# Causal attention on Trainium2: transfers as jobs of their own, in a four-stage transformer block

## The chip, the cores and the metric

The kernel runs on one core of one Trainium2 chip. The metric is device time in microseconds of one execution; the median of the runs is compared. The core's engines are called PE (TensorE, matmuls), DVE (VectorE), ACT (ScalarE), POOL (GpSimd) and SP (SyncE, which here only issues DMAs). Each works through its own instructions in the order in which the program gives them, and waits at an instruction until what it needs is done.

## The reference

The block is a chain of residual stages on x of shape (2, 2048, 256), 4096 tokens of 256 features in float32. Cut to what matters:

```
x = x + 0.5 * moe(layernorm(x))            # mixture of 6 experts, top 2, and a shared expert
x = x + attention0(layernorm(x))           # 16 heads of 16, dense, 2048 x 2048 per head
x = x + 0.5 * moe(layernorm(x))            # the same weights again
x = x + 0.5 * rnn(layernorm(x))            # gated recurrence, then an output projection
x = x + attention1(layernorm(x))           # 16 heads of 16, causal, rotary, relative positions
x = x + 0.5 * rnn(layernorm(x))

def attention1(x):
    q, k = rotary(x @ w_q.T), rotary(x @ w_k.T);  q = q / 4;  v = x @ w_v.T
    rel  = rel_emb[clip(k_pos - q_pos, -32, 32) + 32]          # (L, L, 16)
    s    = q . k  +  q . rel                                   # per head
    a    = softmax(where(k_pos <= q_pos, s, -1e18))
    return (a @ v + sum_k a * rel) @ w_o.T
```

The relative part differs from a constant only in the last 32 keys in front of each query, so the kernel treats a band of 160 columns per 128 queries by itself.

## The kernel before

The token axis is cut into blocks of 512 (TB), of which each batch row has four (SB, named qc for queries), each of four pieces of 128 (CPB, named qb). Heads are taken four at a time (J = 4; G = 4 groups), each in its own 32 rows of PE. One unit of attention work, a group, is (b, qc, g): 32 groups in all. PE writes its products into eight PSUM banks that are handed out in turn by `bank()`, so an engine that is late with emptying a bank stops PE.

*Mixture stages* (`run_moe`). A list written out by hand gives the order of the jobs: `stats(n)` (layer norm statistics on DVE, their reciprocal root on POOL, L96 to L98), `norm(n)` (normalising on DVE, L109, and transposing on PE, L119), `scatter(n)` (eight indirect DMAs issued by POOL, L311, that carry tokens to the places of their experts), `up`, `mul` and `down` for the shared expert. POOL's order is kept as written (`tc.manual_schedule`).

*Attention 0.* A table of jobs by step. Step −1 holds the key products of the first batch row (`keys`: two matmuls on PE, a copy on ACT at L691, eight spread DMAs and eight padding DMAs on SP), then follow, two units per step, `largest` (products of L716 and a row maximum on DVE, L720), and nine steps later `exponential` (L728 on PE, L733 on ACT) and `weighted` (L740 on PE, `gather` at L606 to L611). `vals` computes the values (eight matmuls at L578 for each of eight tiles of a batch row, copied by ACT at L584). For the first row they are jobs of steps 6 to 9.

*`gather`* copies a partial product out of PSUM on ACT (`part`) and adds it to the accumulator `o` on POOL (L611). The first part of a group goes straight into `o`.

*Recurrence* (`recurrence`): the jobs of the layer norm that follows run among its steps.

*Attention 1.* A planner writes lists of steps: `Ms` to `Me` for `largest` of a group (L1055, L1063, L1079), `Es` to `Ee` for its exponentials, `Rs` for its positional product, `By` for the earliest step of its band. Jobs are placed by these. The pieces:

- `rotate` (L960 to L976): a projection on PE, a copy to an `s2` buffer on ACT (L968), a partner swap on DVE (`stream_shuffle`, L970), and multiplications by cos and sin on POOL (L972 to L976). There are four `s2` buffers, shared with other tiles of that size.
- `spread` (L134): eight or four small DMAs on SP that put packed heads into their 32-row groups. `queries` rotates and spreads in one job; `keys` rotates and `keys_out` spreads, both at the same step. `pad_keys` (L141) fills the rest of the rows. The 48 padding DMAs of the later chunks stand before the first step.
- `by_position`: query times relative embedding (L1018), copied by ACT (L1023), stored to DRAM by SP (`skew`, L1025) and loaded back shifted by one column per row (`band`, L1032) in the same job.
- `largest` works on the band (POOL memset L1076 for the first chunk, DVE L1079), takes the maxima off it on POOL (L1093), and with the last of its pieces stores the band to DRAM (`pd`, L1101).
- `positions_load` (L1178) loads the band back unshifted, `positions_exp` (L1186) is its exponential on ACT, `positions_T` and `positions` (L1191, L1197) multiply it by the relative embedding.

All DMAs named here are issued by SP, in the order in which the jobs stand:

```
at(max(By[n], early[n - n % 2] + 2), by_position, n)
at(Rs[n] - 3, positions_load, n)
at(Rs[n] - 2, positions_exp, n)
```

Within a step, half of its jobs run behind the first unit of work and half behind the second.

Of the kernel before, what the change touches and what calls it, by code (L numbers as in the profile page):

```python
# [10 lines left out]
F32 = mybir.dt.float32  # L11
# [6 lines left out]
P = 128  # L18
# [7 lines left out]
TB = 512  # L26
NTB = NT // TB
CPB = TB // P
# [14 lines left out]
def macaron_kernel(ctx: ExitStack, tc: tile.TileContext, t: dict, out: bass.AP):  # L43
    nc = tc.nc
# [121 lines left out]
    def moe(w, ws, gate_w, gate_b, rev, tri, iota, z, behind, last, gathered):  # L166
# [3 lines left out]
        with ExitStack() as s:  # L170
# [14 lines left out]
            def stats(b):  # L185
                if b not in xn and b not in z.mv:
                    z.stats(b)
# [252 lines left out]
            with tc.manual_schedule(engines={mybir.EngineType.Pool}):  # L440
                stats(0)
                stats(1)
                norm(0)
                stats(2)
                norm(1)
                shared_part(0, 0)
                shared_part(0, 1)
                stats(3)
                norm(2)
                shared_part(0, 2)  # L450
                norm(3)
                shared_part(0, 3)
                mul(0)
                stats(4)
                route(0)
                up(1)
                e0 = sort(0)
                stats(5)
                down(0)
                scatter(0)  # L460
                mul(1)
                up(2)
                stats(6)
                up(3)
                scatter(1)
                mul(2)
                norm(4)
                norm(5)
                stats(7)
                scatter(2)  # L470
                scatter(3)
                down(1)
                mul(3)
                down(2)
                norm(6)
                norm(7)
                down(3)
                route(1)
                up(4)
                mul(4)  # L480
                e1 = sort(1)
                down(4)
                up(5)
                mul(5)
                for b in range(HB, NTB):
                    scatter(b)
                down(5)
# [12 lines left out]

                rest(2)
                up(7)
                mul(7)
                rest(1)
                down(6)
                rest(1)
                down(7)
                rest(4)
                if gathered is None:
                    rest(HC)  # L510
# [13 lines left out]
    class Pieces:  # L524
# [76 lines left out]

        def gather(self, t, pv, parts, q0=0):

            if t not in self.o:
                self.o[t] = self.wk.tile([P, TB], F32, name="o")
                nc.scalar.copy(self.o[t], pv)  # L606
                return
            part = self.wk.tile([P, TB], F32, name="part", bufs=parts)
            nc.scalar.copy(part[:, q0:], pv[:, q0:])  # L609
            o = self.o[t][:, q0:]  # L610
            nc.gpsimd.tensor_tensor(o, o, part[:, q0:], ALU.add)  # L611

# [47 lines left out]
    def attention0(norm, tail, wq, wk_, wv, wo, bff):  # L660
# [7 lines left out]
        with ExitStack() as s:  # L668
# [82 lines left out]
            for b in range(B):  # L751
                first = b * SB * G * PER

                for qc in range(SB) if b else ():
                    for c in range(CPB):
                        at(first - 43 + 4 * qc + c, z.ln_stats, b, qc, c)
                    at(first - 37 + 4 * qc, z.ln_transpose, b, qc)
                for qc in range(0 if b else SB):
                    norm.xn.pop(qc)
                    at(-1, z.add_bias, qc)  # L760
                for g in range(0, G, 2):
                    for qc in range(SB):
                        at(first - 7 + PER * g + qc if b else -1, keys, b, g, qc)
                for half in range(2):
                    for qc in range(SB):
                        due = first + 1 + 16 * half + qc
                        at(due if b else 6 + half * 2 + qc // 2, vals, b, half, qc)
            for t, (b, qc, g) in enumerate(groups):
                if t % 2 == 0:
                    at(PER * t - 2, queries, t)  # L770
# [161 lines left out]
    def attention1(norm, tail, w, relk, relv, kbias, dramp, skew):  # L932
# [4 lines left out]
        with ExitStack() as s:  # L937
# [43 lines left out]
            for qc in range(1, SB):  # L981
                for g in range(G):
                    keep_k[qc, g] = z.keep.tile([P, TB], F32, name=f"kT{qc}{g}")
                    pad_keys(keep_k[qc, g])

            def keys(b, qc, g):
                if qc == 0:
                    pair = features_slot()
                for i in range(2):
                    k = kT[b, qc, g + i] = keep_k[qc, g + i] if qc else pair[:, i, :]  # L990
                    if qc == 0:
                        pad_keys(k)
                packed[b, qc, g] = rotate(w["k"], b, qc, g, kbias)

# [7 lines left out]
            def queries(t):  # L1002
                b, qc, g = groups[t]
                z.clear_queries(t)
                xa = rotate(w["q"], b, qc, g, None)
                for i in range(2):
                    spread(q[t + i], xa, i)
                    mx[t + i] = wk.tile([P, CPB, J, MX], F32, name="mx", bufs=2)

            def by_position(t):  # L1010

# [5 lines left out]
                for qb in range(CPB):  # L1017
# [4 lines left out]
                u = wk.tile([P, CPB * J, BAND], F32, name="s2", bufs=4)  # L1022
                nc.scalar.copy(u.rearrange("p a d -> p (a d)"), pr)  # L1023
                flat = skew[t % len(skew)]
                nc.sync.dma_start(  # L1025
                    out=flat.rearrange("s (r w) -> r s w", w=UW)[:, :, P : P + BAND], in_=u
                )
                lead[t] = leads[t % NBAND]
                c = band[t] = lead[t][:, P - BAND :].rearrange(
                    "p (a j k) -> p a j k", a=CPB, j=J  # L1030
# [16 lines left out]
            def largest(t, qb, c, j):  # L1047
# [46 lines left out]
                    band[t][:, qb], band[t][:, qb],  # L1094
                    mneg[:, :, DH : DH + 1].to_broadcast([P, J, BW]), ALU.add,
                )
                if qb < CPB - 1:
                    return

                pd[t] = dramp.tile([CPB * J, P * (BW + 1) + 1], F32, name="pd")  # L1100
                nc.sync.dma_start(  # L1101
# [100 lines left out]
            for n, (b, qc, g) in enumerate(groups):  # L1202
                size = 2 * (qc + 1)
                start = Me[-1] + 1 if n else 0
                free = Es[n - NBAND] + (4 if groups[n - NBAND][1] else 2) if n >= NBAND else -9
                start = max(start, free + 4 - size)
                if n > 5 and n % 2 == 0:
                    start = max(start, Ee[n - 5] + 4)
                Ms.append(start)
                Me.append(start + size - 1)  # L1210
                By.append(max(free, start - 3))
                start = Me[-1] + 2
                if n:
                    start = max(start, Ee[-1] + 1)
                Es.append(start)
                Ee.append(start + size - 1)
                Rs.append(start + (3 if size == 2 else 4))
            largest_at, exp_at = Jobs(), Jobs()
            for n, (b, qc, g) in enumerate(groups):
                for i, piece in enumerate(pieces(qc)):  # L1220
                    largest_at.at(Ms[n] + i // 2, None, n, *piece)
# [3 lines left out]
            at = jobs.at  # L1225
            index = {x_: n for n, x_ in enumerate(groups)}
            early = {
                n: max(Ms[n] - 6, Ee[n - 5] + 1) if n > 5 else Ms[n] - 6 for n in range(0, NG, 2)
            }
            for n in range(NG):  # L1230
                at(Me[n] + 1, z.subtract, n)
            for n in early:
                at(early[n], queries, n)
            for b in range(B):
                for qc in range(SB):
                    f = Ms[index[b, max(qc, 1), 0]]
# [3 lines left out]
                    at(max(f - 12, free), tables, b, qc)  # L1240
                    if b or qc > 1:
                        for c in range(CPB):
                            at(f - 14 + c, z.ln_stats, b, qc, c)
                        at(f - 8, z.ln_transpose, b, qc)
                    for g in range(0, G, 2):
                        f = Ms[index[b, max(qc, 1), g]]
                        at(f - 6 + (qc == 0), keys, b, qc, g)
                        for i in range(2):
                            last_ = Ee[index[b - 1, SB - 1, g + i]] if b and qc else -99
                            at(max(f - 6 + (qc == 0), last_ + 1), keys_out, b, qc, g, i)  # L1250
                    for half in range(2):
                        due = Es[index[b, max(qc, 1), 2 * half]] - 1 + (qc == 0)
                        at(due if b or qc > 1 or half else -2, vals, b, qc, half)
            for n, (b, qc, g) in enumerate(groups):
                at(max(By[n], early[n - n % 2] + 2), by_position, n)
                at(Rs[n] - 3, positions_load, n)
                at(Rs[n] - 2, positions_exp, n)
                at(Rs[n] - 1, positions_T, n)
                at(Rs[n], positions, n)
                end = max(Rs[n], Ee[n] + 1)  # L1260
# [9 lines left out]
            for step in range(min(jobs), max(jobs) + 1):  # L1270
                exps = [a for _, a in exp_at.get(step, ())]
                maxs = [a for _, a in largest_at.get(step, ())]
                todo = jobs.get(step, [])
                for n in range(2):
                    e = exps[n] if n < len(exps) else None
                    m = maxs[n] if n < len(maxs) else None
                    qb = e[1] - groups[e[0]][1] * CPB if e is not None else -2
# [82 lines left out]
    with tc.manual_schedule(engines=ENGINES):  # L1360
# [21 lines left out]
        with ExitStack() as s:  # L1382
# [35 lines left out]
                    n4.turn(cb - 2)  # L1418
                    n4.xn.pop(cb - 2)

            recurrence(rec, n3, False, rest, normals, turns)
        tail = []
        for i, b in enumerate((0, SB)):
            tail += [(3 + 2 * i, n5.stats, b), (4 + 2 * i, n5.normal, b, nc.vector),
# [84 lines left out]
```

## Time and profile before

| | |
|---|---|
| time, median of 3 runs (lowest to highest) | 4228.29 us (4227.61 to 4237.52) |
| profiled execution: its own time, its span | 4239.39 us, 4237.5 us |
| granted PE clock, mean of the span | 0.974 |
| PE busy | 4045.4 us (95%) |
| DVE, ACT, POOL busy | 2696.1, 2499.4, 1696.8 us |

The stages lie one behind the other in the trace: the first mixture at 0 to 420 us, attention 0 at 420 to 2060, the second mixture to 2435, the first recurrence to 2623, attention 1 at 2623 to 4046, and the second recurrence to the end. Times in the trace count from the start of the span. A bracket behind an instruction, such as `[6.42 <-DVE xn L109]`, gives the idle time of its engine before it and the instruction whose end released it. SPq stands for SP's sequencer, which issues DMAs. An instruction has the line of the kernel as printed above; the changed kernel's lines shift by up to 14.

### The profile page before, as it was taken

The numbers are of one execution on the slowest core, as the hardware profiler recorded it, in microseconds if no ns is written. First come the engines' busy times: TensorE is split into PE (matmuls) and PEld (weight loads), VectorE is DVE, ScalarE is ACT, GpSimd is POOL, SyncE is SP. The second block draws the span as 40 slices with busy tenths as digits, with TensorE's granted clock in tenths as the row PEclk, the third lists the DMA queues.
The fourth block names the chain that finished last, engine by engine and source line by source line (L and its number), as shares of the span: only waits on it lengthen the run. The fifth ranks groups of instructions, "written<-read, shape, count | busy, mean of one in ns | idle before, by whom it ended". The sixth has DMA issues, their size and how long they took to land. (4 is left out here: it accounts for less than half of the span.)

```text
span 4237.5 us, 78186 instructions
## 1 busy us (share of the span) xinstructions
PE 4045.4 (95%) x28256; PEld 1952.4 (46%) x28256; DVE 2696.1 (64%) x6122; ACT 2499.4 (59%) x5091; POOL 1696.8 (40%) x1606
## 2 busy tenths in 40 slices
PE   7998999999999999999999988898899999999999
PEld 4664433333344333333356645454454455554445
DVE  6245788888776888888543344665566665666633
ACT  2331788888877888888723231355556665656832
POOL 4244243446333433343362210535535655543510
PEclk9998999999999999999999999899999999999999
DMA  7343000000000000000334201535523444442201
GB/s 245 120 125 86 15 4 4 4 4 4 6 11 14 4 4 4 4 4 12 111 125 126 88 19 36 116 74 100 113 58 65 93 84 100 85 101 41 46 22 40
DMA packets 376881, 245.36 MB, mean 58 GB/s; under 512 B 157232, under 2 KB 349104, under 8 KB 376496
## 3 DMA queue, kind: packets, MB, share of 16 engines
q1 hardware_dynamic: 364208, 206.78, 20.1%
q0 software_dynamic: 12288, 33.57, 2.5%
q8 instruction: 226, 3.70, 0.4%
q14 instruction: 159, 1.30, 0.1%
HBM read 118.36 MB, written 105.12 MB: 53 GB/s over the span
## 5 line engine op out<-in xcount | busy, mean ns | idle before, releaser
L611 POOL TENSOR_TENSOR o<-o,part 128x512 f32<-128x512 f32 (+3 forms) x800 | 964.2, 1206 | 1447.3 <-ACT part L609 1439.4
L720 DVE TENSOR_REDUCE mx<-s 128x1 f32<-128x512 f32 x2048 | 1270.5, 683 | 306.9 <-PE s L716 306.8
L733 ACT ACTIVATE pT<-s 128x512 f32<-128x512 f32 x2048 | 1063.5, 617 | 196.3 <-PE s L716 195.6
L716 PE MATMUL s<-kT,q 32*128 32x512 f32 x4096 | 1030.3, 623 | 11.2 <-DVE mx L720 10.4
L728 PE MATMUL s<-q,kT 32*128 32x512 f32 x4096 | 1011.4, 614 | 0.0
L1161 ACT ACTIVATE pT<-s 128x512 f32<-128x512 f32 (+3 forms) x1280 | 589.8, 541 | 246.3 <-PE s L1140 124.6
L728 PEld LDWEIGHTS s<-q,kT 32*128 32x128 f32 x4096 | 417.3, 183 | 464.4 <-DVE mx L720 325.3
L609 ACT COPY part<-s 128x512 f32<-128x512 f32 (+3 forms) x800 | 467.3, 585 | 277.4 <-PE s L1169 160.4
L1063 DVE TENSOR_REDUCE mx<-s 128x1 f32<-128x512 f32 (+1 forms) x768 | 473.2, 678 | 211.6 <-PE s L1055 190.8
L740 PE MATMUL s<-pT,v 128*32 128x512 f32 x4096 | 549.9, 605 | 0.4
L716 PEld LDWEIGHTS s<-kT,q 32*128 32x128 f32 x4096 | 415.5, 185 | 146.3 <-ACT pT L733 78.3
L1055 PE MATMUL s<-kT,q 32*128 32x160 f32 (+7 forms) x2240 | 339.9, 441 | 22.9 <-ACT part L609 21.5
L1169 PE MATMUL s<-pT,v 128*32 128x512 f32 (+3 forms) x2560 | 313.6, 558 | 22.8 <-DVE mx L1079 13.2
L376 PE MATMUL s<-we,xT 128*128 x592 | 278.9, 593 | 1.1 <-ACT xT L371 1.1
L1079 DVE CUSTOM_DVE_ANT_0 band<-s,band 128x160 f32<-128x160 f32 (+1 forms) x512 | 155.4, 315 | 178.3 <-PE s L1055 76.7
L383 DVE TENSOR_TENSOR h<-sg,s 128x256 f32<-128x256 f32 x148 | 62.3, 421 | 294.8 <-ACT sg L381 294.8
L1055 PE MATMUL s<-b,q 32*128 32x512 f32 (+7 forms) x1280 | 244.3, 520 | 3.5 <-ACT part L609 2.0
L1140 PE MATMUL s<-q,kT 32*128 32x512 f32 (+3 forms) x1152 | 238.9, 512 | 0.0
L740 PEld LDWEIGHTS s<-pT,v 128*32 128x32 f32 x4096 | 82.1, 108 | 335.3 <-ACT pT L733 297.6
L1093 POOL TENSOR_TENSOR band<-band,mneg 128x640 f32<-128x640 f32 x128 | 161.4, 1262 | 174.8 <-DVE mneg L1089 172.4
L423 POOL DMA_INDIRECT yg<-results,at x128 | 125.1, 977 | 239.0 <-DMA results<-y 110.1
L1140 PE MATMUL s<-q,b 32*128 32x512 f32 (+3 forms) x896 | 219.0, 583 | 0.2 <-DVE mx L1079 0.2
(208 smaller groups left out, 5201.1 us busy)
## 6 DMA issues: line engine op xcount, KB each, us to landing
band<-skew SPq DMA_DIRECT2D x32, 1280.0 KB
pd<-band SPq DMA_DIRECT2D x32, 1280.0 KB
xs<-places SPq DMA_DIRECT2D x148, 128.0 KB
results<-y SPq DMA_DIRECT2D x148, 128.0 KB
places<-zero SPq DMA_DIRECT2D x2, 4736.0 KB
we<-in_we SPq DMA_DIRECT2D x12, 768.0 KB
skew<-s SPq DMA_DIRECT2D x32, 256.0 KB
s<-pd SPq DMA_DIRECT2D x32, 256.0 KB
```

The costliest lines, as they stand in the source:

```text
L609: nc.scalar.copy(part[:, q0:], pv[:, q0:])
L611: nc.gpsimd.tensor_tensor(o, o, part[:, q0:], ALU.add)
L716: nc.tensor.matmul(ps, lhsT=q[t][rows(j), ts(qb, P)], rhs=kT[b, g][rows(j), ts(kc, TB)], start=True, stop=True,)
L720: nc.vector.tensor_reduce(mx[t][:, qb * J + j, kc : kc + 1], ps, AX.X, ALU.max)
L728: nc.tensor.matmul(st, lhsT=kT[b, g][rows(j), ts(kb, P)], rhs=q[t][rows(j), :], start=True, stop=True,)
L733: nc.scalar.activation(z.pTs[t, kb, j], st, AF.Exp)
L740: nc.tensor.matmul(pv[rows(j), :], lhsT=v[b, g // 2][:, kb, ds(h * VW, 32)], rhs=z.pTs.pop((t, kb, j)), start=True, stop=True,)
L1055: nc.tensor.matmul(ps[:, ds(cols, n)], lhsT=lhsT, rhs=kT[b, c, g][rows(j), ds(k0, n)], start=True, stop=True,)
L1063: nc.vector.tensor_reduce(m[:, c : c + 1], ps[:, 0:n], AX.X, ALU.max)
L1140: nc.tensor.matmul(ps[:, q0:], lhsT=k, rhs=q[t][rows(j), q0:], start=True, stop=True, skip_group_check=True,)
L1161: nc.scalar.activation(z.pTs[t, kb, j][:, q0:], st.pop((t, kb, j))[:, q0:], AF.Exp)
L1169: nc.tensor.matmul(pv[rows(j), q0:], lhsT=v[b, kb // CPB, g // 2][:, kb % CPB, ds(h * VW, 32)], rhs=z.pTs.pop((t, kb, j))[:, q0:], start=T ...
```

## The change

1. In both mixtures `scatter(1)` goes behind `stats(7)`.
2. `gather` copies the first part of a group into a buffer of the ring of parts, and that buffer then is `o`. The ring is two buffers longer, in place of the two that `o` had.
3. In attention 0, `vals` of the first batch row are jobs of step −1.
4. In attention 1 the 48 paddings go into `keys` of the first row. Transfers become jobs of a second table, `sends`, that counts in half steps and runs ahead of each unit of work: `queries_out` (split from `queries`, which comes a step earlier), `keys_out`, `band_load` (split from `by_position`, whose skew store is now issued by ACT), `band_store` (split from `largest`), `positions_load` and `positions_exp`. Statistics and transposes of the layer norm are placed a step earlier, and the planner keeps a step more between some groups.
5. The first recurrence runs with POOL's order kept as written.

```
 # mixture
-                scatter(1)
                 mul(2)
                 norm(4)
                 norm(5)
                 stats(7)
+                scatter(1)
                 scatter(2)
...
 # gather
+            part = self.wk.tile([P, TB], F32, name="part", bufs=parts + 2)
+            nc.scalar.copy(part[:, q0:], pv[:, q0:])
             if t not in self.o:
-                self.o[t] = self.wk.tile([P, TB], F32, name="o")
-                nc.scalar.copy(self.o[t], pv)
+                self.o[t] = part
                 return
-            part = self.wk.tile([P, TB], F32, name="part", bufs=parts)
-            nc.scalar.copy(part[:, q0:], pv[:, q0:])
...
 # attention 0
-                        at(due if b else 6 + half * 2 + qc // 2, vals, b, half, qc)
+                        at(due if b else -1, vals, b, half, qc)
...
 # attention 1
                     keep_k[qc, g] = z.keep.tile([P, TB], F32, name=f"kT{qc}{g}")
-                    pad_keys(keep_k[qc, g])
...
-                    if qc == 0:
+                    if qc == 0 or b == 0:
                         pad_keys(k)
...
-                xa = rotate(w["q"], b, qc, g, None)
+                packed[t] = rotate(w["q"], b, qc, g, None)
                 for i in range(2):
-                    spread(q[t + i], xa, i)
                     mx[t + i] = wk.tile([P, CPB, J, MX], F32, name="mx", bufs=2)
+
+            def queries_out(t):
+                for i in range(2):
+                    spread(q[t + i], packed[t], i)
...
-                nc.sync.dma_start(
+                nc.scalar.dma_start(
                     out=flat.rearrange("s (r w) -> r s w", w=UW)[:, :, P : P + BAND], in_=u
                 )
+
+            def band_load(t):
+                flat = skew[t % len(skew)]
...
-                if qb < CPB - 1:
-                    return
+
+            def band_store(t):
...
-                start = max(start, free + 4 - size)
+                start = max(start, free + 5 - size)
                 if n > 5 and n % 2 == 0:
-                    start = max(start, Ee[n - 5] + 4)
+                    start = max(start, Ee[n - 5] + 5)
...
-                Rs.append(start + (3 if size == 2 else 4))
+                Rs.append(start + 4)
...
-                n: max(Ms[n] - 6, Ee[n - 5] + 1) if n > 5 else Ms[n] - 6 for n in range(0, NG, 2)
+                n: max(Ms[n] - 7, Ee[n - 5] + 1) if n > 5 else Ms[n] - 7 for n in range(0, NG, 2)
...
                 at(early[n], queries, n)
+                sends.at(2 * early[n] + (2 if early[n] < 0 else 3), queries_out, n)
...
-                            at(f - 14 + c, z.ln_stats, b, qc, c)
-                        at(f - 8, z.ln_transpose, b, qc)
+                            at(f - 15 + c, z.ln_stats, b, qc, c)
+                        at(f - 9, z.ln_transpose, b, qc)
...
-                            at(max(f - 6 + (qc == 0), last_ + 1), keys_out, b, qc, g, i)
+                            due = 2 * (f - 6 + (qc == 0)) + (2 if f < 6 else 3)
+                            sends.at(max(due, 2 * last_ + 2), keys_out, b, qc, g, i)
...
-                at(max(By[n], early[n - n % 2] + 2), by_position, n)
-                at(Rs[n] - 3, positions_load, n)
-                at(Rs[n] - 2, positions_exp, n)
+                e = early[n - n % 2]
+                by = max(By[n], e + (3 if e < 0 else 4))
+                at(by, by_position, n)
+                sends.at(2 * by + 2, band_load, n)
+                sends.at(2 * Me[n] + 3, band_store, n)
+                sends.at(2 * Rs[n] - 6, positions_load, n)
+                sends.at(2 * Rs[n] - 3, positions_exp, n)
...
                 for n in range(2):
+                    sends.run(2 * step + n)
                     e = exps[n] if n < len(exps) else None
...
 # first recurrence
-            recurrence(rec, n3, False, rest, normals, turns)
+            with tc.manual_schedule(engines={mybir.EngineType.Pool}):
+                recurrence(rec, n3, False, rest, normals, turns)
```

More of the change, by code (lines that the diff above doesn't have):

```diff
@@ L1216, in attention1 @@
                 Ee.append(start + size - 1)
-                Rs.append(start + (3 if size == 2 else 4))
-            largest_at, exp_at = Jobs(), Jobs()
+                Rs.append(start + 4)
+            largest_at, exp_at, sends = Jobs(), Jobs(), Jobs()
             for n, (b, qc, g) in enumerate(groups):
```

## The prediction

> **What bounds the kernel now.** I read the busy row of the page first, then the windows of the stages, then the chain of waits of the second attention.
>
> ```profile
> PE 4045.4 (95%) x28256; PEld 1952.4 (46%) x28256; DVE 2696.1 (64%) x6122; ACT 2499.4 (59%) x5091; POOL 1696.8 (40%) x1606
> ...
> 420.00:2060.00 1640.00, 1636.22 (x12890) 620.90 (x12888) 1316.88 (x2215) 1333.36 (x2590) 649.55 (x541) 1.00 0.03 6
> ...
> 2623.00:4046.00 1423.00, 1306.42 (x11411) 688.09 (x11411) 875.09 (x2608) 826.32 (x1759) 693.88 (x639) 0.95 0.40 83
> ```
>
> PE is the bound. The windows' columns are length, busy time of PE, weight loads, DVE, ACT, POOL, then granted PE clock, DMA share, GB/s. The first attention (420 to 2060) leaves nothing to gain: 1636 of 1640 us busy at full clock. The second (2623 to 4046) has 117 us of idle PE and a clock of 0.95. A 5% loss there is not 5% of work: after each gap PE runs at half clock.
>
> ```profile
> 2746.70:2753.50 6.80, 6.78 (x34) 4.40 (x35) 2.48 (x5) 4.33 (x9) 3.74 (x4) 0.51 0.23 71
> 3159.50:3166.40 6.90, 6.85 (x18) 3.22 (x18) 1.35 (x2) 1.96 (x5) 0.72 (x1) 0.50 0.02 7
> 3730.40:3739.80 9.40, 9.37 (x48) 4.47 (x48) 3.44 (x21) 3.34 (x6) 6.48 (x6) 0.50 0.66 140
> 3009.90:3019.50 9.60, 7.43 (x34) 2.55 (x38) 4.42 (x24) 2.13 (x6) 8.68 (x8) 0.50 0.21 46
> ```
>
> Half of each stretch is lost, 3.4 to 4.7 us a gap. What ends the gaps is in the waits (in total, times, longest):
>
> ```profile
> PE s L1018 <- DMA q<-s: 17.0, 1, 17.0
> ...
> ACT s L1186 <- DMA s<-pd: 38.5, 6, 11.9
> ...
> DVE band L1079 <- DMA band<-skew: 34.3, 7, 9.5
> DVE s L970 <- POOL s L976: 24.7, 5, 6.9
> ...
> POOL band L1076 <- DMA band<-skew: 45.9, 6, 12.1
> ...
> SPq L1025 <- ACT s L1023: 192.3, 13, 24.3
> SPq L134 <- POOL s L976: 161.4, 25, 28.8
> ```
>
> Four in-order engines stand behind DMAs, and SP, which issues them, stands at each issue until its source is done (192 us for skew stores, 161 us for spreads). One gap in full, SP first, then ACT, then PE:
>
> ```profile
> 2736.65 4.93 SPq L134 DMA_DIRECT2D kT<-s  x8
> 2741.68 0.53 SPq L1178 DMA_DIRECT2D s<-pd  x1
> ```
> ```profile
> 2745.53 0.63 ACT L1186 ACTIVATE s<-s 128x512 f32<-128x512 f32 x1 [11.88 <-DMA s<-pd]
> ```
> ```profile
> 2746.69 1.46 PE L1154 MATMUL s<-ident,band 128*128 128x128 f32 x4 [9.04 <-ACT part L609]
> ```
>
> The load s<-pd is small but stands on SP behind two sets of eight spreads that waited for the rotation on POOL; ACT's exp of it holds the ACT copies that free PE's banks.
>
> **The change, part by part.** Sums are against the profiled execution (4239.4 us, span 4237.5), 11 us above the median of 4228.3; I carry only the difference over to the median.
>
> *Queue jobs of the second attention.* I followed each PE gap back and grouped them by the engine that stood. Clock loss is half of the half-speed time behind it.
>
> (A) ACT at L1186, as above: gaps 9.04, 5.28, 5.36, 1.95, 7.15 = 28.8, with 14.3 of clock. In the changed program's order 64 or more PE matmuls lie between load and exp (before: 5 to 34). Gone but for a rest: −41.
>
> (B) DVE at L970, whose result needs an s2 buffer that POOL's previous rotation still holds: 3.5, 1.3, 4.2, 2.4, 2.7, 2.1, 1.5, 1.2, 1.2 = 20.2 and 11.6 of clock. Where two rotations fall together, POOL's end and the next shuffle were 4 matmuls apart and are now 8 to 18; but six rotations now wait for spreads to land, since packed queries are held 1.5 steps longer. Two thirds: −22.
>
> (C) POOL at L1076 on the band load of first-chunk groups: 5.8, 7.2 and 4 of clock. Skew store and use stay 25 to 32 matmuls apart, the pd store of another group still ahead on SP: −2.
>
> (D) DVE at L1079 on the band load: 5.5, 2.6, 7.7 and 7 of clock = 23. Distance grows from 31–35 to 67 or more: −20.
>
> (E) One gap at 3241 (POOL late with a layer norm, jobs now a step earlier): −3. The two gaps before 4046 (2.2, 4.2) stay.
>
> New costs: 32 skew stores leave SP for ACT. The nearest rows are the skew issues on SP, 0.36 to 0.53 us when nothing is waited for, 32 × 0.4 = 13 us of ACT; ACT is busy 826 of 1423 us, so this hides behind idle ACT time. But ACT waits with them: in its order 8 places wait for query spreads sent 6 to 18 matmuls before, with the exps behind them and PE behind those. Eight spreads take 5 us to issue; 6 to 18 matmuls last 3 to 9 us. Between 0 and 25, taken 10. Could it gain instead? Only if SP's freed order did, which A and D count. Queries, statistics and transposes a step earlier are the same instructions; only one more step in the plan is added: +3. Waits that this trace cannot show: 0 to 30, taken 10, by the rest of such gaps in B and C. Sum: −88 + 23 = −65.
>
> *Pads.*
>
> ```profile
> 2599.29 29.46 SPq L141 DMA_DIRECT2D kT<-in_pads  x48
> 2628.79 0.42 SPq L960 DMA_DIRECT2D cos<-in_cos  x1
> ...
> 2636.04 5.00 SPq L134 DMA_DIRECT2D q<-s  x8
> ```
>
> The first rotation waits for cos, cos for 48 pads; PE's first L1018 waits 17.0. With the pads behind them, cos is there before the rotation's inputs, q goes out some 10.5 us earlier: −11. The 48 issues (0.62 each, 29.5 us of SP) come back among the early chunks, before the first pd store; SP stands idle there most of the time: +3, at worst +12.
>
> *Scatter after stats(7)*, in both mixture stages:
>
> ```profile
> 74.16 1.04 POOL L98 TENSOR_TENSOR rstd<-ve,mhalf 128x4 f32<-128x4 f32 x1
> ```
> ```profile
> 75.24 1.47 DVE L109 TENSOR_SCALAR xn<-x,mv,rstd 128x256 f32<-128x256 f32 x4 [6.69 <-POOL rstd L98]
> ```
> ```profile
> 75.79 2.29 PE L119 MATMUL s<-ident,xn 128*128 128x128 f32 x8 [6.42 <-DVE xn L109]
> ```
>
> POOL reaches rstd after eight scatters of 1.27 us; ahead of them it ends at 65, before DVE is free for norm(7) at 68.5. PE's 6.4 us go, with 2.1 of half clock here and 1.4 in the second: −8.5 and −7.8. The scatters' sum is unchanged and so is their end, for which the experts' first loads wait; PE may give back 1 each: −14.
>
> *Values of the first batch*, from steps 6–9 to step −1. Key copies on ACT (L691) wait on SP, which spends nearly 9 us on each pair of spreads and pads:
>
> ```profile
> 418.84 0.59 ACT L691 COPY packed<-s 128x512 f32<-128x512 f32 x1 [9.54 <-DMA kT<-in_pads]
> ```
> ```profile
> 402.57 18.62 DVE L720 TENSOR_REDUCE mx<-s 128x1 f32<-128x512 f32 x31 [0.16 <-PE s L716]
> ```
>
> In the changed order PE has 16 key matmuls, then all 64 value matmuls (L578), then the first L716. Eight values need the eight banks of the eight keys, and the last is freed by the copy at 418.84. So no L716 starts before 420, while before 52 of them, with their reductions, lay between 384 and 421. Then 72 L716 units lie before the first exponential (step 9, now at 441); DVE takes 18.62/31 = 0.60 each: 72 × 0.60 = 43, step 9 at 465 with a little start-up. Their POOL memsets run at 382 already; their eight ACT copies (0.59 each) come behind the eight key copies and overlap those reductions. Two values (2 × 1.95) no longer stand after 441: +22, from 15 (values overlap part of it) to 28. Nothing later absorbs it, since that stage is 1636/1640 busy. This part speaks against the change.
>
> *Gather* writes the first part straight into the ring that becomes o: same copies, same number of buffers: 0. What hides a difference is that POOL waits 417 us for parts anyhow; if the ring ran short, PE would wait at L620 (15 us now), 3 us. *POOL's fixed order in the recurrence* leaves POOL's sequence there as it was: 0, no cover needed.
>
> Sum: −65 − 11 + 3 − 14 + 22 = −65; 4228.3 − 65 = 4163.
>
> [...]
>
> **The rivals.**
> *Half of the gain returns as new waits.* DVE waits for spreads holding s2, POOL for first-chunk bands, ACT for skew sources. C and six rotations speak for it; half of 85 (A to D): 4163 + 42 = 4205.
> *Nearly all gaps go.* New costs stay at 3, B wholly goes: 4163 − 20 − 10 = 4133. For it: DMA is 40% busy, so loads land when issued early.
> *The values cost little* (say 3, if banks come free otherwise): 4144. Against it: the order is fixed.
> *Slower: ACT stands at the skew store's source.* Eight places at ACT, each holding exps and PE. Without my 10 for them the sum is 4153; from there to slower by 0.3% (4241) are 88 us, 11 each: 8.6 of wait and 2.4 of clock. At 13 each: 4257. Against it: spreads land within 5 to 9 us, and some lead exists.
> *The change does not do what it says*: true for C, where the order hardly moves; counted.
>
> **How the numbers follow.** Main case 0.53 (own range 4140 to 4190); half returns 0.20; nearly all goes 0.13; values cheap 0.07; slower 0.07. 0.3%, 12.7 us, is about what a measurement of this kernel can tell from no change. Main, cheap and nearly-all are all faster; of half-returns some 0.05 lies above 4215.6, of the slower case 0.02 below 4241. So faster 0.88, same 0.07, slower 0.05. Range 4100 to 4222: the low end takes nearly-all with the low bounds of values and new waits and more of the clock, the high end half-returns with the pads and values at their worst.
>
> **What would show it.** Right: window of the second attention near 1350 at clock 0.97 or more; L1186 no longer in ACT's waits; L1018's wait near 6; no 6.4 gap at L119; the first L728 about 22 us later relative to the first mixture stage's end. Wrong: L728 as early as now; ACT or DVE waiting on DMA q or s for tens of us; gaps on L1169 behind DVE as many as now.

## The result and the profile after

| | before | changed |
|---|---|---|
| median (lowest to highest), 4 runs each | 4231.41 us (4227.61 to 4237.52) | 4170.29 us (4165.43 to 4172.19) |
| ratio, 95% interval | | 0.9852 (0.9835 to 0.9870) |
| span of the profiled execution | 4237.5 us | 4169.4 us |
| mean granted PE clock | 0.974 | 0.979 |

The medians are 61 us apart, the profiled spans 68.1. A fourth run of the kernel before puts its median 3 us above the 4228.3 that the forecast started from. The difference of the spans is split up below, since its parts can be seen. I cut both traces at the same instructions: the first query projection of attention 0, its last L740 (L739 in the changed kernel), the first L814 (L813) of the recurrence, the first L1018 (L1019) and the last L1169 (L1173) of attention 1.

| stretch | before | changed | difference |
|---|---|---|---|
| first mixture, to the first query projection | 357.3 | 349.7 | −7.6 |
| attention 0, to its last weighted product | 1721.7 | 1746.4 | +24.7 |
| second mixture | 342.3 | 334.7 | −7.6 |
| recurrence and prologue, to the first L1018 | 218.6 | 208.5 | −10.1 |
| attention 1, first L1018 to last L1169 | 1397.0 | 1329.5 | −67.5 |
| the rest | 200.5 | 200.6 | +0.1 |

The windows of attention 1, first of before, then of the changed kernel, with the columns of the windows shown earlier:

```profile
2640.01:4036.99 1396.98, 1299.53 (x11383) 683.07 (x11384) 867.92 (x2595) 823.98 (x1755) 691.35 (x637) 0.96 0.40 82
2639.28:3968.75 1329.47, 1286.53 (x11383) 682.04 (x11384) 869.34 (x2594) 824.10 (x1755) 689.33 (x637) 0.97 0.41 87
```

Attention 1 does the same work (11383 matmuls in the stretch, before and after). Its idle PE went from 97 to 43 us, and the half-clock loss, added up over the clock's record in the trace, from 62 to 37. These 80 us are more than 67.5 since part of the half clock lies in idle time.

The waits of attention 1, by engine (us in total, times, longest), first of PE, then ACT, DVE, POOL and SP:

```profile
PE s L1173 <- DVE mx L1083: 12.8, 4, 4.1
PE s L1059 <- ACT part L605: 12.2, 7, 3.1
PE s L1019 <- DVE s L969: 6.3, 1, 6.3
...
ACT part L605 <- DMA q<-s: 18.1, 5, 5.1
...
DVE band L1083 <- DMA band<-skew: 18.6, 4, 5.5
...
DVE s L969 <- POOL s L975: 1.0, 1, 1.0
...
POOL band L1080 <- DMA band<-skew: 50.4, 5, 12.4
...
SPq L1036 <- DMA skew<-s: 285.4, 22, 34.5
SPq L134 <- POOL s L975: 257.3, 27, 29.1
```

ACT's exponential of the positions (38.5 us before, 6 times) has left the list. DVE's wait for POOL at the shuffle is 1.0 us, from 24.7. SP's stands moved more than they shrank: they are longer at the spreads (257 us, from 166) and at the band loads (285, from 100), and gone at the skew stores, which had 390 in all before. What counts is what stands behind SP: its order now has the positions' loads in front. New is the ACT line: five waits for a DMA of q.

### The profile page after: what moved, and what is told of

The parts are those of the page before. It is cut to its first block, busy times and chain, and to the rows that moved or that the text cites. A ratio compares the mean times of both kernels' runs of the same rounds, so it can differ in the third digit from the quotient of the medians.

```text
span 4169.4 us, 78015 instructions
## 1 busy us (share of the span) xinstructions
PE 4036.9 (97%) x28256; PEld 1967.4 (47%) x28256; DVE 2697.1 (65%) x6122; ACT 2498.5 (60%) x5091; POOL 1692.5 (41%) x1606
## 3 DMA queue, kind: packets, MB, share of 16 engines
q1 hardware_dynamic: 298160, 198.39, 18.6%
## 4 chain that ended last, share of the span: by engine, by line
PE 84%; POOL 5%; DVE 4%; DMA 3%; issue 2%; SPq 2%; ACT 1%; ACTq 0%; POOLq 0%; DVEq 0%
PE s L727 13%; PE s L739 12%; PE s L715 10%; PE s L146 8%; PE s L376 6%; PE s L1173 6%; PE s L1059 6%; PE s L1144 5%; PE s L395 3%; DMA band<-skew 2%; PE s L642 1%; POOL places L311 1%; PE s L1154 1%; PE s L1158 1%; PE s L1137 1%
## 5 line engine op out<-in xcount | busy, mean ns | idle before, releaser
L610 POOL TENSOR_TENSOR part<-part 128x512 f32<-128x512 f32 (+3 forms) x800 | 962.6, 1203 | 1407.2 <-ACT part L605 1401.6
L715 PE MATMUL s<-kT,q 32*128 32x512 f32 x4096 | 1031.9, 630 | 0.0
L605 ACT COPY part<-s 128x512 f32<-128x512 f32 (+3 forms) x864 | 506.5, 587 | 287.9 <-PE s L1173 149.7
L739 PE MATMUL s<-pT,v 128*32 128x512 f32 x4096 | 549.9, 605 | 0.4
L715 PEld LDWEIGHTS s<-kT,q 32*128 32x128 f32 x4096 | 426.4, 187 | 125.5 <-ACT pT L732 77.8
L1059 PE MATMUL s<-kT,q 32*128 32x512 f32 (+7 forms) x2240 | 329.6, 433 | 3.6 <-ACT part L605 3.6
L1173 PE MATMUL s<-pT,v 128*32 128x512 f32 (+3 forms) x2560 | 307.9, 549 | 13.1 <-DVE mx L1083 12.8
L739 PEld LDWEIGHTS s<-pT,v 128*32 128x32 f32 x4096 | 82.4, 108 | 335.7 <-ACT pT L732 297.4
```

Source lines behind the costliest of these rows:

```text
L715: nc.tensor.matmul(ps, lhsT=q[t][rows(j), ts(qb, P)], rhs=kT[b, g][rows(j), ts(kc, TB)], start=True, stop=True,)
L739: nc.tensor.matmul(pv[rows(j), :], lhsT=v[b, g // 2][:, kb, ds(h * VW, 32)], rhs=z.pTs.pop((t, kb, j)), start=True, stop=True,)
L1059: nc.tensor.matmul(ps[:, ds(cols, n)], lhsT=lhsT, rhs=kT[b, c, g][rows(j), ds(k0, n)], start=True, stop=True,)
L1173: nc.tensor.matmul(pv[rows(j), q0:], lhsT=v[b, kb // CPB, g // 2][:, kb % CPB, ds(h * VW, 32)], rhs=z.pTs.pop((t, kb, j))[:, q0:], start=T ...
```

## The experiments

There were two kinds of chip in them: on one the kernel before takes 4231 to 4235 us, on the other 4337 to 4340, with nearly all of the difference in the mixtures (399.2 and 392.0 us in `scatter_back` on the second, 357.3 and 342.3 before on the first, in the same order of jobs) and some 10 us in attention 0 (1756.9 in `skew_sync` on the second, 1746.4 in the changed kernel on the first). The text calls them the faster and the slower chip. Ratios are to the kernel before on the same chip, and otherwise only stretches of attention 1 are compared between the two kinds.

**Which of the four parts pays.** The function of attention 1 as a whole put back (`attn1_before`), `scatter(1)` put back ahead of `mul(2)` (`scatter_back`), the values put back, and the skew store back on SP:

```
 # vals_late
-                        at(due if b else -1, vals, b, half, qc)
+                        at(due if b else 6 + half * 2 + qc // 2, vals, b, half, qc)
 # skew_sync
-                nc.scalar.dma_start(
+                nc.sync.dma_start(
                     out=flat...
```

> The changed kernel with the whole function of the second attention as before; mixtures, values, gather and POOL's order in the recurrence stay changed. Theory (the stage windows add up): what is left is -7.6 - 7.6 from the mixtures and +23 to +25 from the values, so 4239, slower than before by 8, although three of its four edits are meant to save; the second attention is worth 69 to 78. Rival (stages interact, the early values also feed the second attention's gain): within 5 of before, or faster.

Measured on the slower chip: 4366.2 us against 4340.5, ratio 1.0053 (1.0037 to 1.0070): slower than before by 26, not by 8. Attention 1 took 1398.3 us, as before, and attention 0 1755.6. Of the 18 us between, 15 are the mixtures', whose gain does not show on this chip (next run). So the other edits, taken together, lose time, and attention 1 carries the whole gain.

> The changed kernel with scatter(1) back ahead of stats(7) in both mixtures. Theory (6.4 us of PE gap and half clock behind it in each): +15, about 4185, 7.6 in each mixture. Rival (the experts' first loads wait for the scatters in either order, so that the gap is paid back there): 4170 to 4173.

Measured on the slower chip: ratio 0.9878 (0.9862 to 0.9895), 4286.9 us. The changed kernel itself was not on this chip, so I compare the mixtures with those of `skew_sync` beside it, which has the new order: 399.2 against 401.3 us in the first, 392.0 against 392.9 in the second. The old order is no slower here; in all seven profiles of the new order on slower chips the two take 398.0 to 402.0 and 392.2 to 396.0. The trace of `vals_late` (new order, same chip) shows where the gain goes. With the new order the 6.4 us in front of L119 are gone, but PE then waits at L210, which transposes what ACT copies at L207, and this copy is late. First PE, then ACT:

```profile
67.68 2.94 PE L119 MATMUL s<-ident,xn 128*128 128x128 f32 x16 [1.28 <-DVE xn L109]
...
84.20 1.11 PE L210 MATMUL s<-ident,lgT 128*128 128x128 f32 x4 [8.28 <-issue]
```
```profile
83.56 0.59 ACT L207 COPY lgT<-s 128x512 f32<-128x512 f32 x1 [12.28 <-remote]
```

The word `remote` says that something outside the profile ended the wait. A second gap of 5.7 us follows at L343. In `scatter_back` the gap at L119 is back and the two places have 2.8 and 2.2 us; its ACT copy stands 8.2 us, `remote` too, and starts at 86.6, only 3 us later than with the new order. On the faster chip the copy waits for PE alone and comes 8.6 us earlier in the changed kernel, at 76.3 instead of 84.9. There the edit pays: `loads_only` below has the old order and takes 357.3 and 342.4 us for the two mixtures, `best1` beside it the new one and 348.7 and 335.9. So the theory holds on one chip; on the other the rival has the time right but not the reason, since PE waits at L210, ahead of the experts. What holds ACT there stays open.

> The changed kernel with the values of the first batch row back at steps 6 to 9. Theory (the 64 value matmuls of step -1 hold PE's banks until the key copies are through, so that no row maximum of attention 0 starts before 415): the first L727 comes 23 to 25 us earlier, the whole is about 4147. Rival (the maxima are bound by DVE and the values only fill a time in which PE would wait anyhow): 4165 to 4170, no change.

Measured on the slower chip: 4266.9 us, ratio 0.9832 (0.9815 to 0.9848). Attention 0, from the first query projection to its last L739, took 1732.5 us against 1756.9 in `skew_sync` and 1757.6 in `scatter_back` on the same chip: the early values cost 24 to 25 us. The first exponential product comes 25.5 us earlier than in `skew_sync`, counted from the first query projection, as the theory has it. In the changed kernel's PE timeline one sees the values paid, groups of 16 waiting for a key copy, and the first L715 behind the last:

```profile
384.02 3.78 PE L578 MATMUL s<-a_v,b 128*128 128x128 f32 x16 [6.02 <-ACT packed L690]
...
401.81 3.72 PE L578 MATMUL s<-a_v,b 128*128 128x128 f32 x16 [5.11 <-ACT packed L690]
411.89 3.78 PE L578 MATMUL s<-a_v,b 128*128 128x128 f32 x16 [6.36 <-ACT packed L690]
415.60 4.99 PE L715 MATMUL s<-kT,q 32*128 32x512 f32 x25
```

> The changed kernel with the skew store issued by SP again, in its job. Theory (SP stands at the store until ACT has copied, with spreads and band loads behind it): 15 to 40 slower, 4185 to 4210, SP's wait at the store over 150 us. Rival 1 [...]: within 5 of 4170. Rival 2 (ACT standing at its store costs more than SP would): 5 to 15 faster, no more waits of ACT on DMA q.

Measured on the slower chip: ratio 0.9887 (0.9863 to 0.9911), 4296.5 us. Attention 1 took 1332.2 us, against 1327.3 in `scatter_back` and 1328.5 in `vals_late`, which both have the store on ACT: 4 to 5 us longer (a third profile with it, `vals_late_2`, has 1330.1). That is the size that the first rival gave, not the theory's 15 to 40. SP did stand at the store as the theory said, 250 us in two rows of its waits, but what it held up was worth little by then. DVE's waits for the band grew (18.6 us in the changed kernel) while ACT's for q went:

```profile
DVE band L1083 <- DMA band<-skew: 33.9, 5, 8.8
```

**Which piece of attention 1 pays.** The kernel before with the positions' load and exponential alone in the new table:

```
-                at(Rs[n] - 3, positions_load, n)
-                at(Rs[n] - 2, positions_exp, n)
+                sends.at(2 * Rs[n] - 6, positions_load, n)
+                sends.at(2 * Rs[n] - 3, positions_exp, n)
...
                 for n in range(2):
+                    sends.run(2 * step + n)
```

> The kernel before with one piece of the change alone: positions_load and positions_exp as jobs of the half-step table, at the half steps of the changed kernel. Theory (A: these loads stood on SP behind spreads, and ACT's exponential of them stopped PE): the second attention is 35 to 45 shorter than before, from the first matmul with the relative embedding to the last weighted product; ACT's wait of 38.5 us at the exponential is under 5; the whole is 0.990 of before. Rival (the load still stands behind spreads of earlier steps that wait for POOL): under 15 shorter.

Measured on the faster chip: 4184.2 us against 4235.3, ratio 0.9881 (0.9864 to 0.9897). Attention 1 took 1343.4 us, 53.6 less than before. The exponential no longer waits for its DMA at all. Laid beside the trace of before at the same matmuls (the n-th of a line in both), the five places of class A give 46 of the 53.6 us (12.5, 9.6, 8.4, 4.4 and 11.2) and the two places of class C, which the edit seems not to touch, 3.9 and 3.1. At C the engines stand as long as before: POOL's waits for the band are 45.6 us (45.9 before), and from the skew product to the division's L620 it takes 23.3 and 24.6 us (23.6 and 24.7). What changed is PE's order. Before, L620 comes straight behind the transposes of L596; in `loads_only`, shown second, a unit of work stands between:

```profile
2899.22 0.66 PE L596 MATMUL s<-ident,mneg 128*128 128x128 f32 x4 [0.57 <-ACT pT L1161]
2905.65 1.11 PE L620 MATMUL s<-ident,o 128*128 128x128 f32 x4 [5.77 <-POOL o L611]
```
```profile
2887.14 1.06 PE L1169 MATMUL s<-pT,v 128*32 128x512 f32 x8 [0.86 <-DVE mx L1079]
...
2891.84 0.66 PE L620 MATMUL s<-ident,o 128*128 128x128 f32 x4 [1.62 <-POOL o L611]
```

Each step's list of jobs is cut in halves. In these steps three jobs became two, so that the division fell into the second half, and PE waits 1.6 us for POOL's sum instead of 5.8. By the planner's rules 15 jobs slide half a step in this way. Classes B and D stayed, as DVE's waits in this kernel's attention 1 show:

```profile
DVE s L970 <- POOL s L976: 44.2, 10, 6.5
DVE band L1079 <- DMA band<-skew: 33.2, 7, 9.3
```

So this kernel has four fifths of attention 1's 67.5 us, 46 by the place of the load and its exponential and 7 by an order that came with it.

**The pads.** The 48 paddings again ahead of the first step:

```
                     keep_k[qc, g] = z.keep.tile([P, TB], F32, name=f"kT{qc}{g}")
+                    pad_keys(keep_k[qc, g])
...
-                    if qc == 0 or b == 0:
+                    if qc == 0:
```

> The changed kernel with the 48 paddings ahead of the first step again. Theory: the first matmul with the relative embedding comes 10 to 12 us later, and the rest of the second attention is 0 to 3 shorter, since the paddings filled idle time of SP: +8 to +12 against the changed kernel. Rival (the paddings among the first bands hold up SP's loads and spreads): the rest is 8 or more shorter, and the whole within 4 of the changed kernel.

Measured on the faster chip: 4178.8 us, ratio 0.9864 (0.9848 to 0.9881). The recurrence with the prologue took 218.9 us (208.5 in the changed kernel), attention 1 1328.4 (1329.5): 10.4 later, then 1.1 shorter. The paddings cost next to nothing where they now are.

**Gather.** Twice, once on the changed kernel and once on `vals_late`, with o in its own two buffers:

> The changed kernel with gather as before (own buffers for o). Theory: nothing within 0.1%; at most the two short gaps at the first divisions of attention 0 (1.75 and 1.53 us, PE waiting for POOL's sum) vanish. Rival (a ring that o shares makes POOL or ACT wait for buffers): 5 or more faster than the changed kernel.

> The base with gather as before. The profile of gather_back had 7 us more in the second attention than the changed kernel, from another chip, which was not expected. Theory (that was the chip or the run): within 3 of the base. Rival (the common ring lets ACT copy the first part of a group without waiting for the accumulator two groups back): 5 to 9 slower than the base.

> The changed kernel with the values back at steps 6 to 9, run again beside the next three, which are all built on it: their common base. Theory: 24 under the changed kernel where the experts are not held up by their DMAs, 0.979 to 0.980 of before; the second attention 1327 to 1331 from the first matmul with the relative embedding to the last weighted product.

`gather_back`: 4177.0 us, ratio 0.9864 (0.9848 to 0.9881), attention 1 1336.8 us. `vals_gather`: 4269.9 us, ratio 0.9846 (0.9832 to 0.9859), against 4264.9 and 0.9833 (0.9819 to 0.9846) for `vals_late_2`; attention 1 1335.6 against 1330.1. In the pair that shares a chip the stretch is 5.5 longer and the medians are 5 apart, though the overlap of the two intervals leaves the latter open. Five profiles with the ring and ACT's store have 1327.3 to 1330.1 in attention 1, the two without the ring 1335.6 and 1336.8, so I count the ring at 5 to 8. In the attention 1 of before it gives nothing, though: `attn1_before` has the ring and takes 1398.3 us, the kernel before 1397.0. Only part can be pointed to: one gap of 2.4 us behind ACT's part copy, with 3.4 us of half clock behind it, is in both kernels without the ring and in none with it. The rest is open.

**Which step freed DVE at the shuffle.** On `vals_late`, queries one step later:

```
-                n: max(Ms[n] - 7, Ee[n - 5] + 1) if n > 5 else Ms[n] - 7 for n in ...
+                n: max(Ms[n] - 6, Ee[n - 5] + 1) if n > 5 else Ms[n] - 6 for n in ...
```

> The base with the queries' jobs six steps ahead of their maxima as before, not seven, so that rotations of keys and of queries fall into one step again. Theory (B: two rotations in one step stop DVE at its shuffle until POOL is through): gaps of 2 to 4 us behind DVE's shuffle return, the second attention 15 to 25 longer than in the base. Rival (what freed DVE was SP's new order, not the step): within 5 of the base.

Measured on the slower chip: 4280.1 us, ratio 0.9862 (0.9847 to 0.9877), 15 over its base `vals_late_2`; attention 1 1341.3 us, 11.2 over it. DVE's waits for POOL are back, at the shuffle and, with the same buffers, at the copy of the transposed positions:

```profile
DVE s L969 <- POOL s L975: 29.7, 8, 4.0
...
DVE s L1197 <- POOL s L975: 15.9, 4, 4.3
```

In the base the first is 1.0 us and the second is not there. So the transfers' table alone does not free B; it takes the queries a step ahead. The step is worth 11 in the stretch (15 by the medians), below the 15 to 25 expected. That is a net figure: the base has five gaps behind ACT's part copy (2.8, 2.7, 1.4, 3.0, 1.4 us), `early6` a single one of 6.0.

**Towards a better kernel.** `best1` has the late values and the skew store on SP as a job half a step behind its copy; `best2` has the late values, ACT's store, and first-chunk groups with a step more of lead:

```
 # best1
+                sends.at(2 * by + 2, skew_store, n)
-                sends.at(2 * by + 2, band_load, n)
+                sends.at(2 * by + 3, band_load, n)
 # best2
-                start = max(start, free + 5 - size)
+                start = max(start, free + 5 - size + (size == 2))
-                By.append(max(free, start - 3))
+                By.append(max(free, start - 3 - (size == 2)))
```

> The changed kernel with the values back at steps 6 to 9 and the skew store issued by SP as a job of its own half a step behind its copy, the band load half a step behind that. Theory (values cost 24; ACT no longer stands at its store behind a DMA of SP: gaps of 2.8, 1.4, 3.1, 1.4 us and some 9 of clock go): 24 + 15 under the changed kernel, 0.976 of before. Rival (SP's order again holds the bands up, half a step later at the least): 24 less what DVE waits more for the bands, 0.979 to 0.984 of before, with more gaps behind DVE at the band.

Measured on the faster chip: 4142.7 us against 4235.3, ratio 0.9783 (0.9767 to 0.9799), the best of all kernels: 92 under before. Attention 0 took 1720.6 us, 26.6 less than `pads_first` beside it: the values. Attention 1 took 1326.7, next to 1327 to 1330 with the store on ACT, so that the store's new place gives next to nothing. The rival was right about the bands: ACT's stands are gone, and DVE's four gaps grew to 6.3, 4.8, 6.3 and 6.1 us.

> The base with one step more ahead of each group of the first chunk: its maxima start a step later and its band is asked for four steps ahead instead of three (four steps more in the plan). Theory (D and C: four gaps of 4.1, 2.8, 3.4, 2.5 us, DVE waiting for the band load, and some 14 of half clock): these gaps go, 15 to 22 under the base, 0.975 of before. Rival (the steps without maxima leave PE short of work, or the wait moves to another group): within 5 of the base.

Measured on the slower chip: 4303.6 us, ratio 0.9917 (0.9903 to 0.9931), 39 slower than its base; attention 1 1366.5 us. The four gaps of PE behind DVE at the band did go, and eight of 3.1 to 7.0 us came, four behind ACT and four behind POOL. In the first place ACT issues the store behind a DMA of keys, and its copy of a part waits 7.4 us (ACT's timeline):

```profile
2960.71 0.59 ACT L1024 COPY s<-s 128x512 f32<-128x512 f32 x1
2968.27 0.39 ACTq L1026 DMA_DIRECT2D skew<-s  x1
2968.70 0.27 ACT L605 COPY part<-s 128x128 f32<-128x128 f32 x1 [7.41 <-DMA kT<-s]
```

and in all, the waits of ACT and of PE in its attention 1:

```profile
ACT part L605 <- DMA kT<-s: 24.2, 4, 7.4
...
PE s L619 <- POOL part L610: 34.4, 9, 7.0
PE s L596 <- ACT part L605: 19.6, 4, 6.0
```

The store reads s2 and writes skew; neither is touched by a spread of keys. The changed kernel has five such stands, behind spreads of q (18.1 us in all). At each of them the store's source was ready: ACT's copy had ended 0.95 to 4.58 us before the store. The semaphores recorded in the changed kernel's trace show what ended the stand. SP's DMAs use eight semaphores there, and ACT's 32 stores use seven of the same eight. At all five stands ACT waits on the semaphore that its store uses, the DMA that used it last was one of SP's spreads of q, and the store follows that spread's landing by 0.07 to 0.08 us. At one of them, for example, the copy ended at 2981.52, the spread was issued at 2982.56 and landed at 2984.42, and the store came at 2984.50. In `best2` the spreads of keys are issued from 2966.33 on, and the store comes at 2968.27, 1.94 us later; at the five stands the spread took 1.86 to 2.68 us from issue to landing. From these times I estimate that it is a stand of the same kind.

The four gaps behind POOL hang on the band loads still. Each ends 5.6 us after POOL's memset got its band, and POOL stands at these memsets 11.8 to 13.9 us for the load (11.7 to 12.7 in the base):

```profile
2993.07 1.11 PE L619 MATMUL s<-ident,part 128*128 128x128 f32 x4 [6.93 <-POOL part L610]
```
```profile
POOL band L1080 <- DMA band<-skew: 56.1, 6, 13.9
```

So the longer lead moved this wait from DVE to POOL. A version with the lead of `best2` and the store of `best1` was not tried.

## Why the prediction was right, and where not

The time lay 7 us over the forecast in the medians (4170.3 for 4163) and inside the range; the change itself was −61 in the medians and −68.1 in the profiles, for −65. The stages came out as forecast, each within 6 us. Within attention 1 the sum was better than its terms, and that is luck: A, C, E and the ring gave some 16 to 19 us more than forecast, B and D some 17 to 21 less. The signs named beforehand came: L1186 has left ACT's waits, L1018's wait is 6.3, the gap at L119 is gone, and the first L728 comes 25 us later, counted from the first query projection.

- *Values, +22.* Measured +24.7 for the whole of attention 0, 24 to 27 by the runs. The mechanism was as written: the first L715 came at 415.6, right behind the values that had waited for the last key copy, and DVE then ran 64 maxima in one piece. The rival in which values cost little fell.
- *Mixtures, −14.* −15.2 on the chip of the forecast, so that less than the 1 us each was given back (0.9 and 0.2). On the other chip nothing. The prediction had no case in which PE waits right behind the gap for something else, here ACT's copy at L207.
- *Pads, −11 and +3.* −10.1 to −10.4, and back about 1.
- *A, −41.* 46 by `loads_only`: right in mechanism, a little small.
- *C, −2.* The places still have gaps in the changed kernel (4.1 and 2.8 us, now behind DVE, for 5.8 and 7.2), and POOL still stands at the band loads, 11.8 and 11.9 us. At the same matmuls they give 2.0 and 1.6 us. That the load would hold as before was right; that PE's order changes there was not foreseen.
- *B, −22.* 11 to 15 by `early6`, net.
- *D, −20.* About 10. Idle time at its three gaps was 15.8 us; two of 3.4 and 2.5 are left in that part of the trace, with as much half clock behind them as before. The longer lead in program order was right, but the band loads behind the four gaps that are left took 13.8 to 14.1 us from issue to landing (one was issued at 2867.9 and landed at 2881.9), so that the lead in matmuls did not close them. At two of D's gaps the load took 6.4 and 6.6 us before and takes 14.1 now: asked for earlier, it also takes longer, against the rival's "loads land when issued early". Why is open.
- *E, −3.* About 7: the gap of 3.4 us went, and the half clock behind it.
- *New costs, 23.* ACT's stands behind q spreads were there, as forecast, at four gaps of PE (2.8, 1.4, 3.1, 1.4 us; half clock for 20 us behind them, 10 lost): some 19 where I took 10. A fifth gap, of 2.7 us with 3.4 of clock, hangs on the same stand behind a load of cos (landed at 2943.78, the store at 2943.88). But `skew_sync` and `best1` show that taking them away gains nothing, since the bands then come later by as much. The prediction treated the stand as a cost of its own; it is the price of the earlier band.
- *Gather, 0.* The step that failed is "same copies, same number of buffers: 0": 5 to 8 in the new attention 1, cause in part open.
- *Recurrence, 0.* Not tried alone; with the pads back (`pads_first`) the stretch with the first recurrence takes 218.9 us, and 218.6 before.
- *SP's stands.* The 192 us given for the skew stores are one of two such rows, the other has 192.8; and the largest row, 304.8 us at the pd stores behind POOL, was left out. Neither entered the sum.

The slower rival, ACT standing at the store's source, did not decide here (18.1 us in five waits), but `best2` shows it deciding: four waits of kT, 24.2 us, next to two of q, 9.0, in a kernel 39 us slower than its base. I had it right that ACT would stand there, and wrong why: at the five stands of the changed kernel the source was ready 0.95 to 4.58 us before the store, and what came last was the landing of a spread of q, 0.07 to 0.08 us before it.

Half clock did not come "after each gap", as the prediction has it. These are windows of the changed kernel, a gap and what follows it, twice:

```profile
2984.00:2985.40 1.40, 0.01 (x1) 0.00 (x0) 0.00 (x0) 0.41 (x2) 0.00 (x0) 1.00 0.24 50
2985.80:2989.20 3.40, 3.40 (x7) 1.62 (x7) 0.50 (x3) 1.53 (x4) 1.69 (x2) 0.50 0.67 113
971.70:973.50 1.80, 0.05 (x5) 0.01 (x1) 1.71 (x3) 1.31 (x3) 1.80 (x3) 1.00 0.00 0
973.50:977.00 3.50, 3.50 (x28) 1.42 (x28) 1.41 (x4) 1.35 (x3) 2.17 (x2) 1.00 0.01 2
```

A gap of 1.4 us was followed by 3.4 us at half clock; one of 1.8 by none. In attention 1 of before, one of 2.6 us that ended at 3638.8 was followed by none either (a clock of 1.00 in the next 6 us). So a gap of under 3 us may or may not cost clock here, and a mean of several is the honest estimate.

## What to carry to other kernels

Look at a DMA's place among the others on its issuer: moving one load of 256 KB and its consumer, which had held ACT for up to 11.9 us, gave 46 of the 67.5 us of attention 1. Where a gap changes that an edit should not touch, compare the order of the program first: 7 us came from a job that slid behind the next unit of work. Ask of each edit in a bundle alone: one that filled PE's early idle time with work blocked the stage's bound for 24 us. An earlier or re-issued transfer can move its wait instead of removing it: with the store back on SP, ACT's waits for q went and DVE's for the band grew from 18.6 to 33.9 us; with a step more of lead, four gaps behind DVE went and eight of 3.1 to 7.0 us came. So a new issuer or a longer lead is to be measured with the engine that now stands.

## What was not expected of the hardware

Stretches at half clock lasted 3.4, 6.8 or 10.2 us in attention 1 of the changed kernel, up to 17.1 where that of before starts, and once 37.5 in the changed kernel (422.4 to 459.9), where attention 0 starts and DVE is busy for 37.2 of them. One of 3.4 us followed a gap of 1.4 us. A DMA that ACT issues stood behind a DMA of SP with which it shared a semaphore and no data: the store at 2984.50, behind the spread of q that landed at 2984.42. Chips of one kind ran each mixture some 40 to 60 us longer than those of the other and attention 1 alike within 2 us, so that the same edit gave 15 us on one and nothing on the other.
